# A graph-attention and top-p diffusion kernel: row loads of the second hop moved to the edges' queue, and transposes of the row blocks set further ahead

## The chip, the cores and the metric

The kernel runs on one core of a Trainium2 chip. Its time is the device time of one execution in microseconds (us). The time before is the median of three runs, 2851.52 us, with the lowest at 2849.42 and the highest at 2852.96. Engines are named as in the profile: PE (matrix multiply), PEld (its weight loads), DVE (vector), ACT (scalar), POOL (GpSimd), SP (the queue that only issues DMAs).

## What is computed

Layer 0 is a graph attention over 4096 nodes with 256 features, added to its input. Layer 1 runs on `h = relu(layernorm(x))` of that result and mixes two diffusions, two steps each. The reference, cut to what matters here:

```python
R = S + eye(N);  R = R / R.sum(-1)          # S is the 0/1 adjacency, 4096 x 4096
for n in range(2):
    A  = top_p_attention(Xa)                # softmax rows cut to their top 90 % and renormalized
    Xf = R @ Xf                             # "hop": graph diffusion
    Xa = A @ Xa                             # "row blocks": attention diffusion
    Z  = Z + Xf @ U1[n].T + Xa @ U2[n].T
out = x + layernorm(X + Z)
```

## The kernel before

**Order of the work.** Everything is written out by hand: inside `manual_schedule` each engine and each DMA queue takes its instructions in the order in which the Python code issues them, and a queue whose head waits holds all that stands behind it. Layer 0 takes the time up to about 800 us. Then, for each step n of layer 1, come one hop over the graph and 32 row blocks. Hop 0 runs up to about 1065 us, the row blocks of step 0 from there to about 1778 us, hop 1 from there to about 2130 us, the row blocks of step 1 to the end.

**A hop** (`hops`, L687) walks over 128 groups: 4 passes over 1024 columns each, times 32 blocks of 128 source rows. For group n it needs three things:

- the source rows, 128 KB. In hop 0 they lie on the chip. In hop 1, `source` (L454) loads them from `xf_d` by a DMA at L461, into a ring of five tiles (three named x1, two named xa);
- the edges, 512 KB from `adj_d`, loaded by `edge` (L472) on SP's queue at L482, into a ring of five tiles (ar, aru);
- the rows split into a rounded part and a remainder, by `split` (L463): one ACT copy (L467) and one DVE subtraction (L468) into a ring of five `hl` tiles.

`graph_products` (L636) then does eight matmuls of 512 columns per group (L646). In round n the loop loads the rows of group n+2, loads the edges of group n, splits row tile n-1, and multiplies group m = n-5. The same rounds take along, one piece at a time, the "fills" of the row blocks to come (projections, first logits, exponentials, probes) and the "picks" (their search for the cut). A fill ends with `first_step` (L968), some twenty small operations in a chain on POOL, which begin by waiting for ACT's probes (L971 to L997).

**A row block** (`attend`, L1154) multiplies one 128 x 4096 block of masked exponentials `e` with the 4096 x 256 features. The PE transposes `e` in eight groups of four 128 x 128 tiles (`turn`, L1121), ACT copies each group from PSUM to an `eT` tile (L1126; two PSUM tiles `tp`, three `eT` tiles), and `gather` (L1129) does four products of 256 columns, which the profile counts as eight matmuls (L1132). In between stand the logits of the block three ahead (`logits`, L758, four chunks of four matmuls, L763) and on ACT their exponentials (L947) and, in groups 3 to 6, four probes (L954). The block ends with `contributed` (L1140, four matmuls of L1142) and, on ACT, with `scaled` (L1134) in step 0 or `weighed` (L1144) in step 1. Before each block `chosen_kept` (L1408) puts the DVE part on its queue: the third probe (L1015), the end of an earlier block (L1310 or L1313), the search (L1033 to L1052), and the mask of `e` (L1058), without which the block's transposes can't start.

The order of one block before, on the PE: logits 0, transposes 0, logits 1, transposes 1, gather 0, logits 2, transposes 2, gather 1, logits 3, transposes 3, gather 2, transposes 4, gather 3, and so on.

Of the kernel before, what the change touches and what calls it, by code (L numbers as in the profile page):

```python
# [56 lines left out]
def gat_then_top_p_diffusion(  # L57
# [18 lines left out]
    nc = tc.nc  # L76
# [4 lines left out]
    NB = N // P  # L81
# [36 lines left out]
    xf_d = dram.tile([NB, P, D], F32, name="xf_d")  # L118
# [43 lines left out]
    with tc.tile_pool(name="l0", bufs=1) as l0, tc.tile_pool(name="l0s", bufs=2) as l0s, tc.tile_pool(name="l0o", bufs=1) as l0o:  # L162
# [26 lines left out]
        with tc.manual_schedule(engines=every | {ET.SP}):  # L189
# [76 lines left out]
            def weighed(b):  # L266
                pm, uv = pro.pm.pop(b), uvs[b % len(uvs)]
                for t in range(2):
                    nc.vector.tensor_mul(uv[:, :, t, :HD], pm[:, :D].rearrange("p (h d) -> p h d", h=H),
                                         uv[:, :, t, HD:].to_broadcast([P, H, HD]))  # L270
# [133 lines left out]
        def evacuate(k):  # L404
# [27 lines left out]
            def sourced(n):  # L432
                source(hop1, n)
                split(hop1, n + 1)
# [14 lines left out]
        order = [(p, j) for p in range(PASSES) for j in range(NB)]  # L449
# [4 lines left out]
        def source(A, n):  # L454
            if n in A.src or n >= len(order):
                return
            if A.hop == 0:
                A.src[n] = X[:, order[n][1], :]
            else:
                A.src[n] = S.rows.tile([P, D], F32, name="x1", bufs=3) if n % 5 < 3 else S.rows.tile([P, D], F32, name="xa")  # L460
                nc.gpsimd.dma_start(A.src[n], xf_d[order[n][1]])  # L461

        def split(A, n):  # L463
            while A.parted < min(n, len(order)):
# [216 lines left out]
        def begin(A, n):  # L681
            for i in range(n):
                source(A, i)
                edge(A, i)
            A.begun = n

        def hops(A):  # L687

            turned = []
            for n in range(A.begun, len(order) + LOOK + 1):  # L690
                if n == A.begun:
                    edge(A, n)
                for i in range(3 if n == A.begun else 1):
                    source(A, n + 2 - (2 - i if n == A.begun else 0))
                edge(A, n)
                m = n - LOOK - 1
                split(A, min(n, m // NB * NB + NB + 2) if m >= 0 and m % NB > NB - 4 else n)
                own(A, m + 3)
                if m >= 0:
                    p, j = order[m]  # L700
                    edge_of_pass = j == NB - 1 or (j == 0 and m > 0)
                    if edge_of_pass:
                        if j > 0:
                            copied, turned = drained(A.hop, p)
                        for c in range(2):
                            for s in range(KC):
                                graph_products(A, m, s, (c,))
                            if j > 0:
                                copied(c, A.acc[c])
                            yield  # L710
                        continue
                    halves = (1,) if m < A.begun else (0, 1)
                    graph_products(A, m, 0, halves)
                    if turned and j > 2 and j % 2:
                        turned.pop(0)()
                    yield
                    graph_products(A, m, 1, halves)
                    yield
# [36 lines left out]
    def bank():  # L755
        return ps2.tile([P, 2, 512], F32, name="mm")[:, 0, :]

    def logits(q, kT, c):  # L758

        pm = ps2.tile([P, 2, 512], F32, name="mm")  # L760
        for t, halves in enumerate(((0, 1), (1, 0))):
            for h in halves:
                nc.tensor.matmul(pm[:, h, :], q[t], kT[:, ds(h * (N // 2) + c * 512, 512)], start=(t == 0), stop=(t == 1))  # L763
        return pm
# [179 lines left out]
    def exponentials(r, c):  # L944

        ev = r.e.rearrange("p (h c n) -> p h c n", h=2, c=4)
        nc.scalar.activation(ev[:, :, c, :], r.pm[c], AF.Exp, bias=r.nm, accum_out=r.sums[:, c // 2, c % 2:c % 2 + 1])  # L947

    def first_probe(r, i):


        h, i = divmod(i, 2)
        void = l1.tile([P, N // 2], I8, name="void")
        nc.scalar.activation(void, r.e[:, ts(h, N // 2)], (AF.Relu, AF.Sign)[i], bias=r.c1, scale=-1.0,  # L954
                             accum_out=r.sums[:, h, 2 + i:3 + i])

    def summed(r):

        void = small.tile([P, 2, 2], F32, name="void4", bufs=2)
        nc.scalar.activation(void, r.sums[:, :, :2], AF.Copy, accum_out=r.z)  # L960
        if r.n == 0:
            one = slice(r.b, r.b + 1)
            up, c1 = col("pulled", 2), col("c1x", 6)
            nc.scalar.activation(up, r.z, AF.Ln, scale=r.G.level[:, one])
            nc.scalar.activation(c1, up, AF.Exp, scale=r.G.pull[:, one], bias=r.c1)
            r.c1 = c1
# [142 lines left out]
    def loads(r):  # L1109
        r.xf, r.part = rows.tile([P, KC, P], F32, name="xf"), rows.tile([P, D], F32, name="part", bufs=3)  # L1110
        nc.sync.dma_start(r.xf, xft_d[r.n][ds(r.b, 1)].rearrange("o p s i -> (o p) s i"))
        if r.n > 0:
            r.v = rows.tile([P, D], F32, name="xa")
            nc.sync.dma_start(r.v, block(v_d, r.b))
            nc.sync.dma_start(r.part, block(z_d, r.b))
            r.x1 = rows.tile([P, D], F32, name="x1", bufs=3)
            nc.sync.dma_start(r.x1, block(x1_d, r.b))
        r.acc = ps1.tile([P, 2, D], F32, name="acc")
        r.far = r.acc[:, 1, :]

    def turn(r, g):  # L1121
        pt = ps3.tile([P, 4, P], F32, name="tp")
        for i in range(4):
            nc.tensor.transpose(pt[:, i, :], r.e[:, ts(4 * g + i, P)], ident)  # L1124
        eT = rows.tile([P, 4, P], F32, name="eT", bufs=3)
        nc.scalar.copy(eT, pt)  # L1126
        return eT

    def gather(r, eT, g, cur):  # L1129
        for i in range(4):  # L1130
            j = 4 * g + i
            nc.tensor.matmul(r.acc[:, 0, :], eT[:, i, :], cur[:, j, :], start=(j == 0), stop=(j == NB - 1))  # L1132

    def scaled(r):  # L1134
        if r.n + 1 < STEPS:
            xa = rows.tile([P, D], F32, name="xa")
            nc.scalar.activation(xa, r.acc[:, 0, :], AF.Copy, scale=r.scale)
            nc.sync.dma_start(block(xa_d, r.b), xa)

    def contributed(r):  # L1140
        for k in range(KC):
            nc.tensor.matmul(r.far, r.xf[:, k, :], S.u1[:, k, :], start=(k == 0), stop=(k == KC - 1))  # L1142
# [5 lines left out]
    def gathered(r):  # L1148
        if r.n + 1 == STEPS:
            nc.gpsimd.tensor_tensor(r.part, r.part, r.v, ALU.add)  # L1150
            nc.gpsimd.tensor_tensor(r.x1, r.x1, ln_b_r, ALU.add)
            nc.gpsimd.tensor_tensor(r.part, r.part, r.xf.rearrange("p k i -> p (k i)"), ALU.add)

    def attend(r, cur, ahead, between={}, eT=()):  # L1154

        if ahead:
            ahead.pm = {}
        def start(c):
            if ahead:
                ahead.pm[c] = logits(ahead.q, ahead.kT, c)  # L1160
                exponentials(ahead, c)
        start(0)
        loads(r)
        r.ri = rinv[:, r.b:r.b + 1]
        last = r.n + 1 == STEPS and r.b + 1 == NB
        if last:
            r.far = bank()[:, :D]
        eT = list(eT) or [turn(r, 0)]
        start(1)
        for g in range(NB // 4):  # L1170
            if g + 1 < NB // 4:
                eT.append(turn(r, g + 1))
            gather(r, eT[g], g, cur)
            if last and g == 4:
                contributed(r)
                weighed(r)
                gathered(r)
            if g < 2:
                start(2 + g)
            elif g == 2 and ahead:  # L1180
                summed(ahead)
            elif g in PROBED and ahead:
                first_probe(ahead, PROBED.index(g))
            if g in between:
                between[g]()
        if not last:
            contributed(r)
            weighed(r)
        scaled(r)
# [193 lines left out]
    for n in range(STEPS):  # L1383
# [4 lines left out]
        with tc.manual_schedule(engines=every):  # L1388
# [3 lines left out]
            for i, _ in enumerate(pieces, 2 * done):  # L1392
                if n > 0 and i % 6 == 1 and i // 6 < NB // 4:
                    g = i // 6
# [54 lines left out]
            for b in range(NB - 1):  # L1449
                chosen_kept(b)  # L1450
                if b + AHEAD < NB:
                    blocks[b + AHEAD] = began(n, b + AHEAD, G)
                attend(blocks[b], cur, blocks.get(b + AHEAD),
                       beside.get(b, {}), [first] if b == 0 else ())
            r = blocks[NB - 1]
# [49 lines left out]
```

## Time and profile before

| what | value |
|---|---|
| median of three runs | 2851.52 us |
| the profiled execution's own time | 2851.36 us |
| its span, first to last instruction | 2849.5 us |
| PE busy | 2794.6 us (98%) |
| DVE busy | 2174.8 us (76%) |
| ACT busy | 1917.7 us (67%) |
| POOL busy | 980.9 us (34%) |
| matmuls of `gather` (L1132) | 4096, 971.7 us |
| transposes (L1124) | 2048, 306.1 us |
| copies to `eT` (L1126) | 512, 297.1 us |
| row loads (L461) | 128 of 128 KB on POOL's queue |
| edge loads (L482) | 256 of 512 KB on SP's queue |
| granted PE clock, mean | 0.994 |

All times are us from the start of the span. Matmuls overlap, and the end that the profile gives for one is modelled; so a PE that is called busy may still be short of its pace. The distance from one matmul's start to the next one's says more.

### The profile page before, as it was taken

To read this page: it belongs to the slowest core of one execution; us is meant where nothing else is said; L and a number is where in the kernel's file an instruction comes from. 1 tells how busy PE (TensorE), PEld (TensorE's weight loads), DVE (VectorE), ACT (ScalarE), POOL (GpSimd) and SP (SyncE) were. 2 spreads that over 40 slices of the span, in tenths; PEclk is the share of its full clock that TensorE was granted. 3 is DMA by queue.
4 is the path that set the end of the run, shared out by engine and by line. 5 is a ranking of instruction groups with operands and counts; after the bars stand their busy time and mean duration, and the time that the engine had idled before them with its cause. 6 is when DMAs were issued, how large, how long until landed. Compare 5 with 4: busy or idle time off the path is not lost. (4 is left out here: it accounts for less than half of the span.)

```text
span 2849.5 us, 51595 instructions
## 1 busy us (share of the span) xinstructions
PE 2794.6 (98%) x18791; PEld 2439.9 (86%) x18791; DVE 2174.8 (76%) x5067; ACT 1917.7 (67%) x3066; POOL 980.9 (34%) x2023
## 2 busy tenths in 40 slices
PE   6999999999999999999999999999899999999998
PEld 5899999999988888888888888667678888888887
DVE  9867878878554485888888887343565999999997
ACT  8867977879533727777887773233427778887782
POOL 7311121111010321333223331111524766666664
PEclk9999999999999999999999999999999999999999
DMA  9969596786376881000000002767891111111110
GB/s 208 261 234 203 215 239 183 226 187 237 116 259 200 261 303 48 25 23 20 20 20 24 23 19 82 240 194 256 272 341 47 31 36 37 31 31 31 36 35 26
DMA packets 161825, 376.43 MB, mean 132 GB/s; under 512 B 18198, under 2 KB 107158, under 8 KB 157462
## 3 DMA queue, kind: packets, MB, share of 16 engines
q1 hardware_dynamic: 124064, 254.33, 27.0%
q0 software_dynamic: 32256, 114.31, 15.5%
q10 hardware_dynamic: 5238, 4.35, 0.5%
q8 instruction: 153, 2.51, 0.4%
q14 instruction: 114, 0.93, 0.1%
HBM read 305.48 MB, written 113.57 MB: 147 GB/s over the span
## 5 line engine op out<-in xcount | busy, mean ns | idle before, releaser
L1132 PE MATMUL acc<-X,eT 128*128 128x256 f32 x4096 | 971.7, 382 | 3.6 <-ACT eT L1126 3.1
L1132 PEld LDWEIGHTS acc<-X,eT 128*128 128x128 f32 x4096 | 738.2, 190 | 111.4 <-ACT eT L1126 31.9
L400 PE MATMUL acc<-ut,m 128*128 128x195 bf16 (+1 forms) x8192 | 698.1, 246 | 1.2 <-DVE m L379 0.9
L400 PEld LDWEIGHTS <-m 128*128 128x128 fp8e4 x8192 | 696.8, 97 | 2.4 <-DVE m L379 1.4
L372 ACT ACTIVATE g<-sr,d_big 128x1024 uint8<-128x1024 f32 x448 | 473.1, 1135 | 10.0 <-DVE m L378 10.0
L947 ACT ACTIVATE e<-mm,nm 128x1024 f32<-128x1024 f32 x256 | 286.3, 1119 | 195.8 <-PE mm L763 195.4
L1126 ACT COPY eT<-tp 128x512 f32<-128x512 f32 x512 | 297.1, 581 | 90.2 <-PE tp L1124 89.8
L1033 DVE MAX8 cand<-big 128x8 f32<-128x228 f32 (+1 forms) x1152 | 348.3, 380 | 0.0
L646 PE MATMUL mm<-ar,hl 128*128 128x512 f32 x848 | 337.7, 409 | 9.7 <-ACT hl L467 3.9
L1015 DVE SCALAR_TENSOR_TENSOR big<-e,c 128x4096 f32<-128x4096 f32 x58 | 261.9, 4515 | 97.6 <-POOL c L1000 58.6
L646 PE MATMUL acc<-ar,hl 128*128 128x512 f32 x848 | 325.3, 394 | 0.0
L1124 PE MATMUL tp<-ident,e 128*128 128x128 f32 x2048 | 306.1, 272 | 1.9 <-DVE ns_i_u L920 1.0
L1124 PEld LDWEIGHTS tp<-ident,e 128*128 128x128 f32 x2048 | 254.8, 140 | 61.2 <-DVE ns_i_u L920 1.3
L378 DVE TENSOR_TENSOR m<-g,ax 128x512 uint32<-128x512 uint32 x256 | 188.8, 737 | 97.3 <-PE acc L400 76.8
L1058 DVE SCALAR_TENSOR_TENSOR e<-e,found 128x4096 f32<-128x4096 f32 x58 | 259.1, 4468 | 0.0
L954 ACT ACTIVATE void<-e,c 128x2048 int8<-128x2048 f32 x128 | 257.5, 2012 | 0.0
L954 ACT ACTIVATE void<-e,c1x 128x2048 int8<-128x2048 f32 x128 | 257.4, 2011 | 0.0
L646 PEld LDWEIGHTS mm<-ar,hl 128*128 128x128 f32 x848 | 160.3, 189 | 50.3 <-issue 10.9
L379 DVE TENSOR_TENSOR m<-m,ax 128x512 uint32<-128x512 uint32 x256 | 183.2, 716 | 25.7 <-PE acc L400 0.5
L763 PE MATMUL mm<-kT,qT 128*128 128x512 f32 x512 | 197.9, 467 | 2.2 <-ACT e L947 2.2
L646 PEld LDWEIGHTS acc<-ar,hl 128*128 128x128 f32 x848 | 160.0, 189 | 36.7 <-issue 4.1
L971 POOL TENSOR_TENSOR sums<-sums 128x2 f32<-128x2 f32 x64 | 12.8, 200 | 511.1 <-ACT void L954 511.1
(313 smaller groups left out, 3610.9 us busy)
## 6 DMA issues: line engine op xcount, KB each, us to landing
ar<-adj_d SPq DMA_DIRECT2D x212, 512.0 KB, 4.5
adj_d<-ax POOLq DMA_DIRECT2D x32, 2048.0 KB, 7.7
ut<-uv_d SPq DMA_DIRECT2D x60, 784.0 KB, 6.1
aru<-adj_d SPq DMA_DIRECT2D x44, 512.0 KB, 4.5
ax<-in_adj_t_dram POOLq DMA_DIRECT2D x32, 512.0 KB, 18.3
x<-xf_d POOLq DMA_DIRECT2D x78, 128.0 KB, 4.6
xf<-xft_d SPq DMA_DIRECT2D x64, 128.0 KB, 2.2
sr<-s_d SPq DMA_DIRECT2D x15, 512.0 KB, 4.8
```

Source lines behind the costliest of these rows:

```text
L372: nc.scalar.activation(g[:, c, :], shared[k].sr, AF.Relu, scale=BIG, bias=d_big[:, h, j:j + 1])
L400: nc.tensor.matmul(shared[k].acc[i][:, t, :cols], m[t][:, c, ts(i, P)], shared[k].ut[j // QUARTER][:, j % QUARTER, t, :cols], start=(j == ...
L646: nc.tensor.matmul(A.acc[c][s], A.hl[m][:, t, ts(s, P)], A.ar[m][:, ts(c, 512)], start=(j == 0 and t == 0), stop=(j == NB - 1 and t == 1))
L763: nc.tensor.matmul(pm[:, h, :], q[t], kT[:, ds(h * (N // 2) + c * 512, 512)], start=(t == 0), stop=(t == 1))
L947: nc.scalar.activation(ev[:, :, c, :], r.pm[c], AF.Exp, bias=r.nm, accum_out=r.sums[:, c // 2, c % 2:c % 2 + 1])
L954: nc.scalar.activation(void, r.e[:, ts(h, N // 2)], (AF.Relu, AF.Sign)[i], bias=r.c1, scale=-1.0, accum_out=r.sums[:, h, 2 + i:3 + i])
L1015: nc.vector.scalar_tensor_tensor(big, r.e, r.c3, r.e, ALU.is_le, ALU.mult, accum_out=r.low3)
L1033: nc.vector.max(cand[:, s, :], big[:, edges[s]:edges[s + 1]])
L1058: nc.vector.scalar_tensor_tensor(r.e, r.e, r.t, r.e, ALU.is_ge, ALU.mult, accum_out=kept)
L1124: nc.tensor.transpose(pt[:, i, :], r.e[:, ts(4 * g + i, P)], ident)
L1126: nc.scalar.copy(eT, pt)
L1132: nc.tensor.matmul(r.acc[:, 0, :], eT[:, i, :], cur[:, j, :], start=(j == 0), stop=(j == NB - 1))
```

## The change

Three edits, the first in the hop, the others in `attend`:

- the load of the source rows (L461) is issued on SP's queue, the one that takes the edges (L482), in place of POOL's;
- the first group of transposes stands ahead of the first chunk of logits; the second group stands ahead of the second chunk;
- inside the loop, group g transposes for group g+2 in place of g+1.

```diff
@@ source
-                nc.gpsimd.dma_start(A.src[n], xf_d[order[n][1]])
+                nc.sync.dma_start(A.src[n], xf_d[order[n][1]])
@@ attend
+        eT = list(eT) or [turn(r, 0)]
         start(0)
         loads(r)
         r.ri = rinv[:, r.b:r.b + 1]
         last = r.n + 1 == STEPS and r.b + 1 == NB
         if last:
             r.far = bank()[:, :D]
-        eT = list(eT) or [turn(r, 0)]
+        eT.append(turn(r, 1))
         start(1)
         for g in range(NB // 4):
-            if g + 1 < NB // 4:
-                eT.append(turn(r, g + 1))
+            if g + 2 < NB // 4:
+                eT.append(turn(r, g + 2))
             gather(r, eT[g], g, cur)
```

The rings keep their sizes. The PE's order in one block becomes: transposes 0, logits 0, transposes 1, logits 1, transposes 2, gather 0, logits 2, transposes 3, gather 1, logits 3, transposes 4, gather 2, and so on. On SP's queue, round n now issues the rows of group n+2 and then the edges of group n.

## Prediction

> **What bounds the kernel now.** First the page: shares and the forty slices.
>
> ```profile
> span 2849.5 us, 51595 instructions
> PE 2794.6 (98%) x18791; PEld 2439.9 (86%) x18791; DVE 2174.8 (76%) x5067; ACT 1917.7 (67%) x3066; POOL 980.9 (34%) x2023
> ...
> PE   6999999999999999999999999999899999999998
> ```
>
> The PE is full nearly everywhere; between the first slice and the last, one alone shows an 8 (1995 to 2066 us, near the end of hop 1). So what the change can win lies in holes inside the PE's own stream. In the row blocks I look for them in the waits of 1150 to 1700 us, then in the PE's timeline of one block (start, length, line, form).
>
> ```profile
> PEld acc L1132 <- ACT eT L1126: 12.6, 49, 0.3
> ```
>
> ```profile
> 1446.58 1.89 PE L1132 MATMUL acc<-X,eT 128*128 128x256 f32 x8
> 1448.31 0.60 PE L1124 MATMUL tp<-ident,e 128*128 128x128 f32 x4
> ...
> 1455.49 0.60 PE L1124 MATMUL tp<-ident,e 128*128 128x128 f32 x4
> 1456.10 1.99 PE L1132 MATMUL acc<-X,eT 128*128 128x256 f32 x8
> ```
>
> ```profile
> 1448.74 3.74 PE L1132 MATMUL acc<-X,eT 128*128 128x256 f32 x16
> ...
> 1773.90 3.62 PE L1132 MATMUL acc<-X,eT 128*128 128x256 f32 x16
> ```
>
> Two waits per block, both for an `eT` copy. Four transposes move the start on by 0.436 (four steps of 0.109); gather 0 came 0.61 after, so 0.17 late, and its eight matmuls took 1.99 against 1.89, so 0.10 more. The last two gathers took 3.74 beside four probes, 3.62 in a block without: 0.12. Sum 0.39 us a block in step 0. In step 1 gather 0 starts 0.56 after its transposes (2473.54 to 2474.10), 0.12 late, again 1.99 long, and the end again 3.74: 0.34.
>
> Then hop 1 in windows of 10 us, and POOL and ACT in it.
>
> ```profile
> 2020.00:2030.00 10.00, 10.00 (x45) 8.24 (x44) 8.22 (x25) 6.21 (x9) 8.76 (x20) 1.00 0.93 341
> 2030.00:2040.00 10.00, 5.17 (x19) 3.41 (x19) 5.09 (x22) 4.12 (x8) 3.89 (x11) 0.78 0.83 288
> 2040.00:2050.00 10.00, 6.64 (x24) 4.97 (x23) 2.73 (x15) 0.40 (x1) 6.69 (x15) 0.84 0.53 163
> ```
>
> ```profile
> 2018.95 0.28 POOL L971 TENSOR_TENSOR sums<-sums 128x2 f32<-128x2 f32 x1
> ...
> 2027.58 0.34 POOL L997 TENSOR_SCALAR c<-fell,c,up 128x1 f32<-128x1 f32 x1
> 2028.02 0.63 POOL L461 DMA_DIRECT2D xa<-xf_d  x1
> ...
> 2044.66 1.72 POOL L461 DMA_DIRECT2D x<-xf_d  x3
> ```
>
> ```profile
> 2033.59 0.40 ACT L467 CAST hl<-xa 128x256 fp32r<-128x256 f32 x1 [6.56 <-DMA xa<-xf_d]
> ...
> 2049.39 0.40 ACT L467 CAST hl<-x 128x256 fp32r<-128x256 f32 x1 [9.73 <-DMA x<-xf_d]
> ```
>
> In each window the PE is second; the last three numbers are its clock, the DMA share and GB/s. POOL holds the row loads back behind `first_step` (L971 to L997), twice, to 2028.02 and 2044.66; the copies then wait 6.56 and 9.73 us for rows; the PE falls to half, while DMA engines stand idle. So rows issued late are the limit there, not bandwidth.
>
> **What the Trainium skill says.** "TensorE: Matmul & The Clock Gate", section What's actually happening: an idle window of about 3.4 us halves the PE's clock until it has been busy again. The trace agrees: after the holes matmuls start 0.43 apart in place of 0.23, and the clock column shows it. "DMA: Bandwidth & Descriptors", section Queues, rings and completion order: each DMA engine takes turns between the queues with work, and goes in order within one. So a row load on SP's queue stands behind edges issued before it, and ahead of those after. The trace shows the two queues apart only: 512 KB of edges land in 4.5 us (median), rows on POOL's queue in 4.6, 128 KB loads on SP's queue in quiet stretches in 2.2. "SBUF — State Buffer", section SBUF: two separate sides: DVE and POOL lock each other out of a shared port for whole instructions. In step 1 POOL's L1320, one element a partition, takes 4.36 beside the mask L1058, and DVE's L1045 takes 0.70 (0.32 in step 0) beside POOL's L1152. It matters below.
>
> **The rows' loads.** Removed: 128 issues of 0.54 us on POOL. They hide in POOL's idle time, worth nothing by themselves. Added: 128 issues on SP at 0.43 (x1 loads there now), 0.86 per group with the edges, under the 1.83 us that eight matmuls take: hidden. What is gained: from 2031.86 to 2056.17 the PE starts 46 matmuls, 46 x 0.2286 = 10.5 us, in 24.3. Loss 13.8, of which about 4.3 is half clock. On SP the loads no longer wait for ACT's probes, so all of it goes.
>
> Three new costs. (a) Order on SP: the rows of n+2 wait for the split of n-3, and behind them stand the edges of n, which wait for products n-5. Split n-3 starts when products n-8 free its `hl`, three groups or 5.5 us earlier; 0.8 for copy and subtraction and at most one 2.35 us DVE search (L1009) in front leave 2.3 us. Cost 0. If an edge did go out later: it has four groups, 7.3 us, to land and needs 4.5, so 2.8 us of cover. (b) The first groups after the step's branch: rows 5 to 7 left POOL at 1773.6 to 1776.3 before; now they stand behind the edges of group 5, issued at 1784.5, so rows 5 go out near 1784.9, land 2.2 to 3.5 later and need 0.85 of splitting, against products 5 at 1788.15: 0 to 1.1 late, and edges 6 go out 1.7 later. Bounds 0 to 4; I take 1. (c) Bandwidth: 640 KB (655360 bytes) per 1.83 us is 358 GB/s. From 2101 to 2126 the PE ran without a hole at 367 GB/s and DMA share 1.01, but over the hole-free 100 us to come the lead in edges can run dry. Above 364 (367 / 1.01) there is no loss; at 350, 2% of 100 us. Bounds 0 to 6; I take 1.5. A gain beyond the holes is excluded: the rest of the hop runs at the PE's pace. Net 13.8 - 2.5 = 11.3.
>
> **The transposes.** Nothing is added or removed, only moved. Gather g now needs a copy whose transposes ended two gathers earlier (3.9 us, before 2.17); ACT's copy plus probe, 2.5 us a group in place of the PE's 2.17, runs four groups behind by at most 1.3, so the wait of 0.12 at the end goes. The two `tp` tiles make transposes g+2 wait for copy g, which is as old as that: no wait. The three `eT` tiles need gather g-1, just done on the same engine. At the start: transposes 0 end 0.6 after the block before (with the tail of the matmul), ACT's `xa` ends near 0.7 (step 1: `xf` and the normalization near 1.2), copy 0 by 1.3 to 1.8; transposes 2 want it at 2.73. Logits 2 want the first exponential (near 2.8) at 4.9. So the 0.17 + 0.10 goes too. One more step from transposes to logits costs 0.02.
>
> The transposes move ahead of 0.93 us of logits that used to cover the mask. In step 0 the mask ends 4.6 us before the last matmul of the block ahead starts: still covered. In step 1 it ends 2.05 before. What is late next there: DVE shows no wait and looks like the bound, but its L1050 ends at 2480.90, 0.07 after POOL's L1333 (2480.83), a lock each block. Its loop: mask end 2468.97, POOL free 1.21 later, POOL's chain 10.26, then 0.47, then 9.93 to the next mask end: 21.87. The PE comes to 22.26 - 0.34 + 0.02 = 21.94. So DVE follows by a hair, and the mask's lead shrinks to about 1.6 us: cost 0.
>
> Step 0: 22.305 (L1015 from 1126.78 to 1706.70, 26 blocks) goes to 21.94: 0.37 x 29 blocks with logits = 10.7. Step 1: 0.32 x 29 = 9.3. The last three blocks of each step wait for `eT` 0 or for DVE's mask (gaps of 0.57, 0.84, 1.04) as before: 0. Sum 20.0; between 12 (DVE holds step 1 at 22.2) and 22.
>
> **Sum.** 2851.36 (the profiled execution, 1.9 outside its span) - 11.3 - 20.0 = 2820. The median of the runs shown is 0.16 above it; I predict 2820.
>
> **Rivals.**
> - DVE bounds step 1: for it, no DVE wait and 97 us busy in 100; against it, the lock on POOL. Step 1 gives 1: 2828.
> - The hop's gain is eaten by bandwidth: for it, DMA share 1.01 at the end; then it gives 2: 2829. Against it, 400 GB/s in 2090 to 2100.
> - Slower: SP's queue holds the edges. If the wait for a split (head of the queue) made each edge issue w late, a group's cycle of five edge tiles would take (1.83 + 4.5 + w) / 5, over 1.83 from w = 2.8. Over some 55 groups without fills, the 34 us of gains are gone at w = 5.9; at 6.5 the loss is (12.83 / 5 - 1.83) x 55 = 41, so 2851.4 - 34 + 41 = 2858. Against it: the split would have to be 8 us later than (a) has it.
> - Transposes stay tied to ACT's copies (the move shifts the wait from gather to transposes): then only the hop gains, 2840.
>
> **Chances.** Forecast (2814 to 2826) 0.72; DVE bound 0.09; bandwidth 0.09; tied to ACT 0.03; slower 0.04; within 0.2% 0.03. The range 2813 to 2832 takes in the first three. A measurement of this kernel tells about 0.2% from no change.
>
> **What would show it.** Right: no wait of L1132 for `eT` in blocks 1 to 27, blocks 21.9 apart in both steps, the PE at 10 of 10 and full clock from 2020 to 2050 in the hop, no row load on POOL. Wrong: DVE steps above 22.1 in step 1, waits of transposes for copies, edge waits in the hop, or holes of over 3 us behind the branch.

## The result and the profile after

| | before | after |
|---|---|---|
| median of the runs (us) | 2851.53 (4 runs, 2849.42 to 2852.96) | 2819.80 (4 runs, 2818.34 to 2821.59) |
| ratio, 95% interval | | 0.9888 (0.9873 to 0.9902) |
| profiled execution, its span | 2851.36, 2849.5 | 2820.09, 2818.1 |
| hop 0 begins, then to the first gather of step 0 | 780.7, 294.7 | 781.2, 295.2 |
| step 0, first to last gather matmul | 701.7 | 690.2 |
| hop 1, first matmul to the first gather of step 1 | 362.3 | 351.5 |
| hop 1, first to last matmul of L646 | 359.8 | 348.5 |
| step 1, first to last gather matmul | 701.7 | 691.6 |
| distance of two blocks (L1015), step 0 and step 1 | 22.309, 22.268 | 21.912, 21.913 |

The time fell by 31.7 us to 2819.8; the forecast was 2820. The rows below the third are starts of matmuls and of L1015, read from the two traces; the distances are means over some twenty blocks of each step. By the rows that end at a gather, hop 1 gave 10.8 us, step 0 11.5, step 1 10.1, and 1.0 came back ahead of step 0. But the first gather of a step now stands behind one more group of transposes: it starts 2.95 us after the hop's last L646, 2.49 before. So these rows count 0.5 us too much for each step and as much too little for the hop in front of it. Cut at the last L646, hop 1 gave 11.3, step 0 11.1, step 1 9.6, and 0.6 came back ahead of step 0.

These parts come from one trace of each kernel. From first to last L646, hop 1 took 356.7 to 360.4 us in the five traces where it is that of the kernel before (before, runs 2, 3, 4 and 10), and 347.4 to 349.7 in the five where it is that of the kernel after (after, runs 1, 6, 7 and 11). Hop 0 began between 780.7 and 782.2 in all thirteen traces, though no run changes what stands ahead of it.

The page after, with the lines that answer to those of before:

```profile
span 2818.1 us, 51577 instructions
PE 2772.0 (98%) x18791; PEld 2443.1 (87%) x18791; DVE 2164.6 (77%) x5067; ACT 1925.4 (68%) x3066; POOL 907.2 (32%) x1895
...
PE   6999999999999999999999999999999999999998
```

The 8 inside the PE's row is gone. The PE's share is 98% as before: a share doesn't show this change, because the modelled end of each matmul had covered most of the holes in the row blocks (before, the PE counts as busy for 399.64 of the 400 us from 1200 to 1600). The waits from 1150 to 1690 us (engine, line, what it waited for, us in all, times, longest):

```profile
POOL sums L971 <- ACT void L954: 328.1, 25, 13.2
ACT e L947 <- PE mm L763: 62.8, 49, 1.4
DVE big L1015 <- POOL c L1000: 37.8, 25, 1.5
ACT xa L1137 <- PE acc L1142: 18.4, 25, 0.7
ACT e L947 <- POOL den L980: 9.7, 24, 0.4
```

The list is complete and names no wait of the PE; before, L1132 waited 48 times for `eT` in this stretch. The list of 2220 to 2730 us, in step 1, names none either. The PE's timeline over one block's boundary (start, length, line, matmuls):

```profile
1441.43 5.35 PE L1132 MATMUL acc<-X,eT 128*128 128x256 f32 x24
1446.61 1.03 PE L1142 MATMUL acc<-u,xf 128*128 128x256 f32 x4
1447.48 0.60 PE L1124 MATMUL tp<-ident,e 128*128 128x128 f32 x4
...
1450.21 0.60 PE L1124 MATMUL tp<-ident,e 128*128 128x128 f32 x4
1450.65 1.89 PE L1132 MATMUL acc<-X,eT 128*128 128x256 f32 x8
```

Gather 0 starts 0.44 after the transposes ahead of it (0.61 before) and takes 1.89 (1.99 before). The last gathers have no transposes between them now, so 24 matmuls stand in one row: 5.18 us to the start of the next line, 0.216 each. Both pieces of the old wait are gone.

Hop 1 in three windows, of which the second and the third showed 5.17 and 6.64 us of PE before (us, busy time and instructions of PE, PEld, DVE, ACT, POOL, then clock, DMA share, GB/s):

```profile
2020.00:2030.00 10.00, 10.00 (x46) 8.21 (x45) 8.71 (x38) 3.13 (x8) 6.00 (x17) 1.00 1.01 371
2030.00:2040.00 10.00, 10.00 (x46) 8.21 (x45) 9.96 (x18) 2.13 (x6) 0.00 (x0) 1.00 1.00 372
2040.00:2050.00 10.00, 10.00 (x46) 8.21 (x44) 9.52 (x31) 2.21 (x6) 0.00 (x0) 1.00 0.99 341
```

There are 46 matmuls in 10 us at full clock, where the last two windows had 19 and 24 before; the DMA engines are as full as the PE. Two places with holes remain in the hop (beside three waits of 0.4 near 1965, which were there before), the first just behind step 0's last block:

```profile
1773.73 3.82 PE L646 MATMUL acc<-ar,hl 128*128 128x512 f32 x16
1778.54 0.49 PE L646 MATMUL mm<-ar,hl 128*128 128x512 f32 x1 [0.99 <-ACT hl L467]
1780.31 0.50 PE L646 MATMUL acc<-ar,hl 128*128 128x512 f32 x1 [1.27 <-DVE ar L490]
...
1781.58 0.63 PE L646 MATMUL mm<-ar,hl 128*128 128x512 f32 x1
1782.01 0.63 PE L646 MATMUL acc<-ar,hl 128*128 128x512 f32 x1
```

```profile
2065.24 0.47 PE L646 MATMUL mm<-ar,hl 128*128 128x512 f32 x1 [1.29 <-DMA ar<-adj_d]
...
2102.92 0.47 PE L646 MATMUL mm<-ar,hl 128*128 128x512 f32 x1 [0.72 <-issue]
```

The first two holes are the rows late behind the branch: the second waits for DVE's L490, which ran at 1779.97, behind the split of the last of these rows. From 1781.5 the clock is halved for 3.4 us, and matmuls start 0.43 apart. The hole of 1.29 ends with edges that landed 8.5 us after their issue, where DMA runs at 401 GB/s and share 1.04 (2060 to 2066). POOL had just issued four stores of 256 KB (L663, from 2054.78 on); what part of the hole is theirs, no run shows. The hole of 0.72 ends with DVE:

```profile
2099.93 2.35 DVE L1009 SCALAR_TENSOR_TENSOR e<-e,found 128x2048 f32<-128x2048 f32 x1
...
2102.20 0.42 DVE L468 TENSOR_TENSOR hl<-xa,hl 128x256 fp32r<-128x256 f32 x1
2102.54 0.28 DVE L490 TENSOR_TENSOR ar<-ar,ident 128x128 fp32r<-128x128 f32 x1
```

The row that L468 splits there had landed at 2101.18; the split stood behind a search.

### The profile page after: what moved, and what is told of

The parts are those of the page before. It is cut to its first block, busy times and chain, and to the rows that moved or that the text cites. A ratio compares the mean times of both kernels' runs of the same rounds, so it can differ in the third digit from the quotient of the medians.

```text
span 2818.1 us, 51577 instructions
## 1 busy us (share of the span) xinstructions
PE 2772.0 (98%) x18791; PEld 2443.1 (87%) x18791; DVE 2164.6 (77%) x5067; ACT 1925.4 (68%) x3066; POOL 907.2 (32%) x1895
## 3 DMA queue, kind: packets, MB, share of 16 engines
q0 software_dynamic: 26112, 97.53, 13.8%
## 5 line engine op out<-in xcount | busy, mean ns | idle before, releaser
L1132 PE MATMUL acc<-X,eT 128*128 128x256 f32 x4096 | 948.0, 379 | 0.0
L1132 PEld LDWEIGHTS acc<-X,eT 128*128 128x128 f32 x4096 | 748.1, 190 | 85.7
L646 PE MATMUL mm<-ar,hl 128*128 128x512 f32 x848 | 336.4, 407 | 3.8 <-DMA ar<-adj_d 1.7
L1015 DVE SCALAR_TENSOR_TENSOR big<-e,c 128x4096 f32<-128x4096 f32 x58 | 261.4, 4506 | 87.0 <-POOL c L1000 56.9
L646 PE MATMUL acc<-ar,hl 128*128 128x512 f32 x848 | 324.1, 393 | 1.3 <-DVE ar L490 1.3
L971 POOL TENSOR_TENSOR sums<-sums 128x2 f32<-128x2 f32 x64 | 12.7, 199 | 623.7 <-ACT void L954 622.2
L646 PEld LDWEIGHTS mm<-ar,hl 128*128 128x128 f32 x848 | 159.6, 188 | 43.7 <-issue 9.5
L646 PEld LDWEIGHTS acc<-ar,hl 128*128 128x128 f32 x848 | 159.3, 188 | 37.7 <-issue 4.1
```

The costliest lines, as they stand in the source:

```text
L646: nc.tensor.matmul(A.acc[c][s], A.hl[m][:, t, ts(s, P)], A.ar[m][:, ts(c, 512)], start=(j == 0 and t == 0), stop=(j == NB - 1 and t == 1))
L1015: nc.vector.scalar_tensor_tensor(big, r.e, r.c3, r.e, ALU.is_le, ALU.mult, accum_out=r.low3)
```

## The experiments

Eleven kernels ran. The first five and the tenth are edits of the kernel before, the others of the kernel after. "Before" in each is the kernel before on the same chip. The kernel after was timed in the result above alone, so the runs built on it are set against it by their ratios and traces.

**1. The rows' loads alone.**

```diff
-                nc.gpsimd.dma_start(A.src[n], xf_d[order[n][1]])
+                nc.sync.dma_start(A.src[n], xf_d[order[n][1]])
```

> The rows' loads on the edges' queue alone, the transposes as before. My theory: the rows stood behind first_step on POOL; the two holes near 2035 and 2048 us and their half clock go, 13.8 us, less about 2.5 of new cost (behind the branch, and bandwidth): 2840, hop 1 shorter by 10 to 12 us, the blocks' distance still 22.3 and 22.26. Rival (the parts need one another, since the row blocks gain only if the fills come earlier): under 8 us. Rival (bandwidth eats it): under 5 us.

Measured: 2840.69 against 2849.52, ratio 0.9969 (0.9957 to 0.9982). Hop 1 took 350.1 us, 12.2 less; the distances stayed at 22.308 and 22.258, and L1132 waited for `eT` 48 times as before. The PE is full from 2020 to 2050, and the middle window reads:

```profile
2030.00:2040.00 10.00, 10.00 (x46) 8.21 (x45) 8.08 (x36) 3.88 (x7) 6.32 (x17) 1.00 0.99 350
```

So the queue alone gives the hop's part and nothing else.

**2. The transposes alone.**

```diff
+        eT = list(eT) or [turn(r, 0)]
         start(0)
...
-        eT = list(eT) or [turn(r, 0)]
+        eT.append(turn(r, 1))
         start(1)
...
-            if g + 1 < NB // 4:
-                eT.append(turn(r, g + 1))
+            if g + 2 < NB // 4:
+                eT.append(turn(r, g + 2))
```

> The transposes' two edits alone, the rows' loads still on POOL. My theory: 2851.5 - 20.5 = 2831, blocks 21.92 apart in both steps, hop 1 with its two holes as before. Rival (DVE bounds step 1): the second step's distance near 22.2 and 2841.

Measured: 2829.74 against 2849.52, ratio 0.9932 (0.9915 to 0.9948). The distances are 21.910 and 21.912, those of the whole change. Hop 1 took 360.0 and kept its holes, with the clock halved for 6.8 us:

```profile
2020.00:2030.00 10.00, 5.57 (x20) 3.85 (x19) 6.55 (x28) 4.12 (x8) 4.54 (x12) 0.83 0.78 281
```

The gains of runs 1 and 2, 8.8 and 19.8, add up to 28.6 of the 31.7, which is within the intervals of the two ratios (each about 4 us wide). In the traces the hop's part (12.2 in run 1) and the steps' (20.7 in run 2, without the 0.5 that each step owes to the place of its first gather) make 32.9, and run 1's execution lost 1.7 to a clock halved for 3.4 us in step 1.

**3 and 4. The two moves of the transposes, each alone.** In run 3 the first group stands ahead of the first logits, and the loop stays one group ahead; in run 4 the first group stays where it was, the second goes ahead of the second logits, and the loop runs two ahead.

```diff
+        eT = list(eT) or [turn(r, 0)]
         start(0)
...
-        eT = list(eT) or [turn(r, 0)]
         start(1)
```

> Only the first group of transposes ahead of the first logits; the loop still one group ahead, rows on POOL. My theory of two separate waits: the wait of gather 0 goes (0.27 a block in step 0, 0.22 in step 1), the wait of the last gather (0.12) stays: blocks 22.04 and 22.04 apart, 58 x 0.245 = 14 us, 2837. Rival (one cause, ACT being late for the whole block): either all of it goes (2831) or next to nothing (2850).

```diff
         eT = list(eT) or [turn(r, 0)]
+        eT.append(turn(r, 1))
         start(1)
...
-            if g + 1 < NB // 4:
-                eT.append(turn(r, g + 1))
+            if g + 2 < NB // 4:
+                eT.append(turn(r, g + 2))
```

> Only the loop two groups ahead; the first transposes still behind the first logits, the second behind the second, rows on POOL. My theory: the wait of the last gather (0.12) goes, the wait at the start stays and is now seen at transposes 2, which need the tp tile of copy 0: blocks 22.18 and 22.14 apart, 58 x 0.12 = 7 us, 2844.5. Rival (two groups of lead cover the start as well): 2831. With e3 it must add up to e2.

Measured in run 3: 2834.47, ratio 0.9946 (0.9929 to 0.9962), distances 22.022 and 22.027. In run 4: 2842.42, ratio 0.9972 (0.9960 to 0.9983), distances 22.140 and 22.081. What is left of the wait in each, from the waits of 1150 to 1680 us of run 3:

```profile
PEld acc L1132 <- ACT eT L1126: 6.2, 24, 0.3
```

and from those of 1150 to 1690 of run 4:

```profile
PEld tp L1124 <- ACT eT L1126: 6.2, 24, 0.3
```

One wait a block is left in each, half of the two before. The one of run 4 has moved from the gather to the transposes: started late, group 0 is copied late, and group 2 wants its `tp` tile. Run 4 gained 0.04 to 0.06 a block more than expected, so the wait seems to cost less there than in front of the gather. In step 0 the two moves gave 0.287 and 0.169, together 0.456 against 0.397 for both at once; they overlap by 0.06, and are otherwise independent.

**5. Rows on POOL's queue, with nothing in front of them.** The kernel before, with the hop-1 `first_step` of POOL cut to one operation (the first step of the search and the repair of step 1 are left out). The diff leaves out the definition of `one_step`.

```diff
...
-                first_step(blocks[b - 1])
+                (first_step if n == 0 else one_step)(blocks[b - 1])
...
-        repaired(R, cur)
+        if n == 0:
+            repaired(R, cur)
```

> The kernel before, rows' loads still on POOL's queue; for the three blocks whose fills run beside hop 1, first_step is one POOL operation in place of nineteen (their limit is then the first guess), and the repair of step 1 is left out, so only the hop is to be read. My theory (the loads stood behind that chain): the holes near 2035 and 2048 us go and hop 1 falls from 362 to about 349 to 351, rows on POOL or not. Rival (POOL's queue itself is slow to bring rows): holes stay, hop 1 at 358 or more.

Measured in one run: 2835.26 against 2849.82; hop 1 took 347.7 us, and 345.3 from first to last L646, less than in any trace where all rows are loaded on SP. The three big holes are gone, and from 2020 to 2050 the PE is busy for 29.92 of 30 us:

```profile
2030.00:2040.00 10.00, 10.00 (x45) 8.21 (x44) 7.26 (x24) 2.04 (x5) 2.16 (x4) 1.00 1.00 376
```

So POOL's queue is no slower in itself: what cost 14.6 us (362.3 - 347.7) was `first_step` in front of the loads. The kernel after needs 3.3 more than this run from first to last L646 (348.5 - 345.3), by the five traces of that hop 2.2 to 4.5. Not all of that need be SP's doing: run 5 also has less work on POOL, beside which DVE's instructions stretch (run 6), and no run parts the two.

**6. The kernel after without POOL's last two operations of a block in step 1** (the product with `ln_g` and the sum with `x`; left out of the result). In spite of its label it is built on the kernel after.

```diff
-            nc.gpsimd.tensor_tensor(r.part, r.part, ln_g_r, ALU.mult)
-            nc.gpsimd.tensor_tensor(r.part, r.part, r.x1, ALU.add)
```

> The kernel after without the two last POOL operations per block of step 1 (the gain by ln_g and the addition of x1 are left out, so the output lacks them). My theory: DVE was locked to POOL's chain and not the bound; time and blocks' distance as in the kernel after (2820, 21.91), and DVE, freed of the lock, now shows waits or less busy time in step 1 (96 in 100 falls to 93 or less). Rival (DVE sets step 1 in the kernel after): the distance falls below 21.8, 2816 or less.

Measured: 2817.59, ratio 0.9883 (0.9867 to 0.9900); the kernel after had 0.9888. The distance stays at 21.913, as expected; step 1 is 1.5 us shorter, and the mask's lead over the last matmul of the block ahead grows from 1.5 to 3.0. But DVE's busy time in 400 us of step 1 is 388.34, against 388.43 in the kernel after, and no wait of DVE appears. That part of the expectation failed, and the timelines say why. First the kernel after, DVE and then POOL:

```profile
2474.47 0.36 DVE L1045 TENSOR_TENSOR_SCAN cum<-best,cum,zero 128x48 f32<-128x48 f32 x1
2474.86 0.60 DVE L1049 TENSOR_SCALAR drop<-cum 128x48 f32<-128x48 f32 x1
2475.50 0.79 DVE L1050 CUSTOM_DVE_ANT_0 work<-drop,best 128x48 f32<-128x48 f32 x1
```

```profile
2465.96 0.20 POOL L971 TENSOR_TENSOR sums<-sums 128x2 f32<-128x2 f32 x1 [0.16 <-ACT void L954]
...
2475.49 0.73 POOL L1334 TENSOR_TENSOR part<-part,x 128x256 f32<-128x256 f32 x1
```

Then run 6, DVE and POOL:

```profile
2473.55 0.67 DVE L1050 CUSTOM_DVE_ANT_0 work<-drop,best 128x48 f32<-128x48 f32 x1
```

```profile
2465.40 0.20 POOL L971 TENSOR_TENSOR sums<-sums 128x2 f32<-128x2 f32 x1 [1.66 <-ACT void L954]
...
2473.43 0.74 POOL L1152 TENSOR_TENSOR part<-part,xf 128x256 f32<-128x256 f32 x1
```

L1050 takes 0.27 where POOL is idle. In the kernel after it ends (2476.29) with POOL's L1334 (2476.22); in run 6 with L1152 (2474.22 and 2474.17). With less work on POOL, DVE runs ahead until it meets the operations that are left, and its stretched instructions fill the time again. POOL can't start earlier: L971 now waits 1.66 for ACT's probe, which follows the PE.

**7. Seven of eight groups a block.** The kernel after; the last eighth of the features is left out of every block. Many rows are then repaired at the end, so only distances can be read, not the total of 3250 us. The diff leaves out that `gather` takes its last block as an argument.

```diff
...
-        for g in range(NB // 4):
-            if g + 2 < NB // 4:
+        for g in range(NB // 4 - 1):
+            if g + 2 < NB // 4 - 1:
...
-            gather(r, eT[g], g, cur)
+            gather(r, eT[g], g, cur, NB - 4)
```

> The kernel after with seven of eight groups of transposes and gather in every row block (the last eighth of each row is left out of the sum): 2.17 us less PE work per block. My theory: step 0 falls to DVE's own work, 20.5 apart; step 1 stays near 21.87, the loop of mask, POOL's chain and search: in all about 2770. Rival (no such loop, DVE's own work bounds it too): step 1 at 20.9 to 21.1, in all 2745. Rival (PE still): 19.75 in both, 2705.

Measured: 20.303 in step 0, 21.965 in step 1. With an eighth of the PE's work gone, step 0 fell by 1.6 and step 1 not at all. DVE and then POOL there:

```profile
2311.64 0.81 DVE L1045 TENSOR_TENSOR_SCAN cum<-best,cum,zero 128x48 f32<-128x48 f32 x1
2312.49 0.70 DVE L1049 TENSOR_SCALAR drop<-cum 128x48 f32<-128x48 f32 x1
2313.23 0.27 DVE L1050 CUSTOM_DVE_ANT_0 work<-drop,best 128x48 f32<-128x48 f32 x1
```

```profile
2302.92 0.20 POOL L971 TENSOR_TENSOR sums<-sums 128x2 f32<-128x2 f32 x1
...
2312.42 0.73 POOL L1334 TENSOR_TENSOR part<-part,x 128x256 f32<-128x256 f32 x1
```

L971 waits for nothing, and L1049 ends (2313.19) with L1334 (2313.15). POOL's chain starts when the mask ends, and DVE goes on when the chain ends. In step 1 of this run the clock of the PE was halved for 3.4 us in every second or third block. That isn't what holds the step: the distances average 21.971 with a halved clock and 21.961 without.

**8. Rows 5 to 7 issued ahead of the branch.** The kernel after, with three row loads of hop 1 put in front of the work at the end of step 0 that issues edges.

```diff
-                beside.update({2: lambda: (both_weights(), begin(second, 5)), 5: lambda: split(second, 2), 6: lambda: (split(second, 5), own(second, 5))})
+                beside.update({2: lambda: (both_weights(), begin(second, 5)), 5: lambda: split(second, 2), 6: lambda: (split(second, 5), own(second, 5), [source(second, n) for n in (5, 6, 7)])})
```

> The kernel after, with the rows of groups 5 to 7 loaded in the last block of step 0, ahead of the branch, in place of behind the edges of group 5. My theory: the two holes behind the branch (0.99 and 1.27 us) go, hop 1 from 351.5 to 349.3, 2817.6, too little for the clock and to be read from the trace. Rival (edges 6 were late there, not rows): the holes stay.

Measured: 2816.44 (2814.86 to 2817.20), ratio 0.9879 (0.9862 to 0.9895); hop 1 took 349.3. The PE behind the branch:

```profile
1777.10 0.51 PE L646 MATMUL mm<-ar,hl 128*128 128x512 f32 x1 [0.21 <-issue]
...
1781.00 0.47 PE L646 MATMUL mm<-ar,hl 128*128 128x512 f32 x1 [0.89 <-DMA ar<-adj_d]
```

The two holes that waited for rows are gone, and the clock isn't halved; a hole of 0.21 is left, and one of 0.89 that waits for the edges of the group behind them, landed at 1780.86. It computes all that the kernel after does. In the traces it is 2.9 us shorter (span 2815.2 against 2818.1), 2.2 of it in the hop. The intervals of the two ratios overlap, and the hop's 346.4 from first to last L646 lies only 1 us below the shortest of the five traces whose hop is that of the kernel after. So that the row holes went is shown; that the kernel is faster by 2 to 3 us is not shown.

**9. Fewer rows.** The kernel after, where two of five groups of hop 1 use the rows of the group before.

```diff
-            if A.hop == 0:
+            if A.hop > 0 and n % 5 in (1, 4):
+                A.src[n] = A.src[n - 1]
+            elif A.hop == 0:
```

> The kernel after, but in hop 1 two of every five groups use the rows of the group before them, so 51 of the 128 row loads are left out (that part of the result is computed from other rows). A group then moves 589 KB on average in place of 655, 322 GB/s at the pace of the PE in place of 358. If the holes of 1.29 us near 2064 and 0.72 near 2102 that hop 1 still shows come from bandwidth, they vanish, those of 0.99 and 1.27 behind the branch stay or shrink, and hop 1 goes from 351.5 to 349.5. If they come from the order on SP's queue or from the fills, they stay and hop 1 stays at 351 to 351.5. Row blocks unchanged, 21.91 apart. Span 2816 against 2818.

Measured in one run: 2817.31, span 2814.5; hop 1 took 348.1, 3.4 less than in the kernel after, of which some 1.7 (half of 3.4) is the clock. (A group moves 603 KB on average, 330 GB/s at the PE's pace; the 589 above counts in another unit than the 655.) The hole of 1.29 became 0.60, that of 0.72 is gone, those behind the branch are 0.81 and 0.84 and no longer halve the clock. From 2060 to 2066 the DMA engines are still full (405 GB/s), from 2080 to 2100 they move 327 GB/s where the kernel after moves 354. The holes of the later hop come to 1.4 to 2.0 us in the five traces whose hop is that of the kernel after, and that of 0.72 is missing in runs 6 and 11 too. With 0.60 in all, run 9 lies below the five, so the rows have a part in these holes. Whether by their bytes, by their places on SP's queue or by the time of their splits, this run doesn't tell.

**10. The kernel before without POOL's last two operations** (those of run 6, left out of the result).

```diff
-            nc.gpsimd.tensor_tensor(r.part, r.part, ln_g_r, ALU.mult)
-            nc.gpsimd.tensor_tensor(r.part, r.part, r.x1, ALU.add)
```

> The kernel before, without the last two POOL operations of a block in step 1 (the product with ln_g and the sum with x, L1332 and L1333, 1.54 us; left out of the result). If DVE's lock on POOL set the distance of step 1 before, it falls from 22.27 by up to 1.5, to no less than the PE's own 21.9, and the time falls by 10. If the PE's two waits for eT set it, as the prediction says, the distance stays at 22.25 to 22.27, the mask's lead grows by about 1.5, and the time falls by less than 2: 2850.

Measured: 2848.22 against 2850.17, ratio 0.9994 (0.9985 to 1.0003). The distance of step 1 is 22.254, the mask's lead 4.0 in place of 2.05, and DVE is busy for 388.86 of 400 us. DVE there (POOL's L1152 ends at 2476.43):

```profile
2474.38 0.74 DVE L1050 CUSTOM_DVE_ANT_0 work<-drop,best 128x48 f32<-128x48 f32 x1
2475.05 0.08 DVE L1050 DVE_READ_ACCUMULATOR2_ANT found<- 128x1 f32 x1
2475.16 0.63 DVE L1051 TENSOR_SCALAR work<-drop 128x48 f32<-128x48 f32 x1
2475.82 0.67 DVE L1052 CUSTOM_DVE_ANT_0 work<-best,work 128x48 f32<-128x48 f32 x1
```

DVE didn't bound step 1 before: with 1.5 us taken off its partner the block got 0.014 shorter, and three stretched instructions take up the time.

**11. Seven groups, without POOL's last two operations.** Runs 7 and 6 together, the same parts left out.

> The kernel after with seven of the eight groups of every row block (the last eighth of the features left out) and without the last two POOL operations of step 1 (1.55 us a block). As in the run with seven groups the total includes repairs and says nothing; only distances of L1015 are to be read. Loop of DVE and POOL: step 1 goes from 21.97 to 21.97 - 1.55 = 20.4; step 0 stays at 20.30. If step 1 with seven groups was held by something else, it stays at 21.9 to 22.

Measured in one run: 20.303 in step 0, 20.959 in step 1. So the loop of run 7 was the bound, and a shorter chain on POOL releases it, by 1.0 and not by the whole 1.55 that was expected. No instruction is stretched any more, and DVE's own work is the bound:

```profile
2406.98 0.19 DVE L1049 TENSOR_SCALAR drop<-cum 128x48 f32<-128x48 f32 x1
```

That work is that of step 0 plus 0.66: L149 and L150 (0.43 and 0.18 with the gaps) exist in step 1 alone.

## Why the prediction was right

**The row-block waits (0.39 and 0.34 a block): right.** The distances fell by 0.397 and 0.355, to 21.912 and 21.913 where 21.94 stood. Both waits vanished, run 2 shows that the move alone does it, and runs 3 and 4 split it into the start (0.287 in step 0) and the end (0.169). The 0.02 that I added for one more step from transposes to logits did not show: the distance fell by slightly more than the waits. Step 0 gave 11.1 for 10.7, step 1 9.6 for 9.3 (cut at the last L646 of the hop). The lead of 3.9 us between transposes and gather was that of the last gather but one; the last has 3.46 (two gathers, 16 matmuls at 0.216), which was enough. The last three blocks kept their gaps, as said, only that the one of 0.57 now stands in front of transposes.

**Hop 1 (net 11.3): right, 11.3 from first to last L646, with its terms slightly off.** (The mean of the five traces of each kind gives 10.3.) The loss of 13.8 was real and was POOL's chain: run 5 takes the chain away, leaves the queue alone, and wins 14.6. The three new costs came to about 3.3 where 2.5 stood. Order on SP (a), taken as 0: edges took 4.7 us to land (4.5 before; these are medians of both hops, in hop 1 alone 5.1 and 5.0), and no hole goes back to a split in front of them. The branch (b), taken as 1: about 2.2, by run 8 (1 to 3 by the five traces). This term was mis-sized because I counted one late group and left out the clock: there were two holes (0.99 and 1.27), of which run 8 took 1.2 away, and a halved clock behind them, about 1.7 (half of 3.4), which it took away too. The two make more than 2.2, since waits for edges grew elsewhere in run 8. Bandwidth (c), taken as 1.5: later holes of 2.0, of which run 9 took 1.4 away; but only the one of 1.29 ended with a DMA, and the other stood behind a DVE search such as (a) has in it. (b) and (c) can't be told apart to a tenth, since run 9 also shrank the holes behind the branch. The bound of 364 GB/s is 363 (367 / 1.01); nothing hangs on it.

**DVE in step 1: right in what it did, loosely right in why.** The mask's lead became 1.49 (1.6 was said), and DVE follows. The loop exists: 21.965 in run 7, released in run 11. It has no fixed length. The 21.87 had POOL end beside L1050, as in the kernels before and after; in run 7 it ends beside L1049, and L1050 (0.27) is still to come: 1.05 from the mask's end to POOL's chain, 10.23 of chain, 0.74 from there to L1015 in place of 0.47, and 9.94 to the next mask's end. In the kernel after the loop has a little room, since POOL's L971 still waits for ACT's probe, 2.3 us in some 24 blocks, 0.1 each; so the PE sets 21.91. A further gain of the PE in step 1 would be lost, as run 7 shows: with 2.17 us less on the PE the step came to 21.965, no less than 21.912.

**The rivals.** "DVE bounds step 1" fell by runs 2, 6 and 10: distances of 21.912 with POOL's operations and without. "Tied to ACT's copies" fell by run 2, though run 4 shows that it is real with half of the change. "Bandwidth eats the hop's gain" would have cost 9 us of it; the holes that can be put down to it are 2.0 at most. "SP's queue holds the edges" didn't come about: run 1 alone is faster, and its windows from 2020 to 2050 are full.

**The share of luck.** The forecast missed by 0.2 us, its parts by up to 0.6: hop 1 gave what was said, the steps 0.7 more, and 0.6 was lost ahead of step 0, most of it before hop 0 begins, where traces of unchanged code differ by 1.5. Inside the hop two errors of 0.8 cancelled: the loss removed was larger than said, and so were the new costs. And hop 1 of one and the same code differs by up to 3.8 us from trace to trace. So the mechanism was right, and the closeness of the total is luck.

## What to carry to other kernels

Loads that the matrix engine needs belong on a queue in which no long chain of other work stands in front of them; before moving them, ask which of the new queue's waits they will stand behind, and issue the first few ahead of a branch. If a product waits for a copy out of PSUM, look at both ends of the loop (how far the first group is ahead, how far the loop runs ahead): each wait was worth its own share here, and running the loop further ahead without an earlier start shifted the wait at the start to the buffer (run 4). Do not read a bound from a busy share: take work away from the suspected partner, and see whether the distance of two blocks moves.

## What the runs showed of the hardware

**A busy share of 97% said nothing about DVE.** In 400 us of step 1 DVE was busy for 388.8 (before), 388.4 (after), 388.3 (run 6), 388.9 (run 10), 388.5 (run 7) and 388.2 (run 11), at distances of 22.27, 21.91, 21.91, 22.25, 21.97 and 20.96. It was the bound in the last two only, in run 7 together with POOL. The Trainium skill's "SBUF — State Buffer", section SBUF: two separate sides, says that only the port pair shared by DVE and POOL brings engines into conflict; the runs agree (0.19 and 0.27 became 0.60 to 0.79 and ended within 0.08 of POOL's instruction), and add that an engine with slack slides until it meets its partner, so that the slack appears as busy time.

**About half a window of idle time halved the PE's clock.** In the kernel after, holes of 0.99 and 1.27 us, with one matmul between them, were followed by 3.4 us at half clock; in run 11, 0.74 and 1.48 were too. In run 1, 1.33 and 0.84 were not, nor 0.81 and 0.84 in run 9. The Trainium skill's "TensorE: Matmul & The Clock Gate", section What's actually happening, speaks of one idle window of about 3.4 us, and of a window that runs freely. The window agrees: in each of the thirteen traces, every change of the clock behind the first 60 us stands on a grid of 3.413 us, to within 6 ns. The idle time does not, and the measurement decides. Those traces hold some 10,200 cells of their grids at full clock (behind the first 100 us, and ahead of the repairs of runs 7 and 11). All 24 cells in which the PE was idle for 1.89 us or more were followed by half clock, and none with less than 1.68; of six from 1.68 to 1.81, two were. So the limit lies near half a window, and it counts where on the grid a hole falls. The cell of the kernel after, from 1778.14, was idle for 1.68 us; in run 1 the two holes fell into two cells, one each, and nothing came of them. In the kernel before one hole of 1.80, in the cell from 2032.18, was enough, so there the spacing of matmuls agrees with the prediction's reading of the page and the length of the hole doesn't. Idle time is known through the modelled ends of matmuls, so the limit is an estimate.
